# First expert weights, cleared sums and tables issued from the second scored tile of the first routing on

## Chip, cores and metric

The kernel runs on one core of one Trainium2 chip. The metric is the device time of one execution in microseconds (us). Before the change it is 1562.98 us, the median of three runs (1562.39 to 1564.65).

## What is computed

The reference is a block of three parts on X of 4 x 512 tokens with 512 channels: a mixture of experts, attention, and the same mixture of experts again. Cut to what matters:

```python
x = x + 0.5 * ffn(layernorm(x))        # "layer 0"
x = x + attention(layernorm(x))        # attn has its own layernorm, rope and residual
x = x + 0.5 * ffn(layernorm(x))        # "layer 1", same weights
# ffn: scores = sigmoid(x @ gate_w); 4 of 8 groups, then 6 of 64 experts a token;
#      every expert takes at most 96 tokens; out = silu(x @ w_gate) * (x @ w_up) @ w_down
#      plus one shared expert for all tokens (ws_gate, ws_up, ws_down)
```

All of it is in float32. The 2048 tokens are 16 tiles of 128 rows, in 4 groups (one for each batch entry) of 4 tiles.

## The kernel before

Layer 0 has two stages: the routing, and the experts. The change lies in the first.

**Routing of layer 0** (lines 633 to 719). For each tile t a chain of small steps is issued, which the text below calls by one letter and the tile's number:

- `row` (L289): ScalarE writes the normalised tile xn (L295, two buffers), and SyncE stores it to the DRAM table xn_d (L297). A third `row` needs a buffer whose store has landed.
- `turn` (L300): TensorE transposes xn (L201), ScalarE copies the result out as xT (L202).
- `score` (L305): TensorE multiplies by the gate weights (L308), ScalarE applies tanh (L313, tile lgs).
- `choose(g)` (L315): a chain of some 40 small VectorE instructions for the four tiles of a group, from sb (L323) to the weights wt (L397). wt shares the buffer of sb, so the next group's sb (L323) waits until SyncE has stored wt(g) to xn_d (L516).
- `count`, `digits`, `tokens`, `spread` (L400 to L458): they turn the choice into slot lists; TensorE's L447 needs VectorE's V and A (L423, L427).
- `gate`, `turn_h`, `down` (L477, L494, L502): the shared expert; TensorE L208, ScalarE L211, VectorE L214 and L215, TensorE L508, VectorE L509.

The routing begins with a first loop of nine rounds (lines 653 to 667), each `row(t)`, `turn(t)`, `score(t-1)`, with `choose(0)` after score 3. Then comes the main loop (lines 694 to 716): in each of its 15 rounds it runs the shared expert of one tile, the first steps of a tile two groups ahead, and one entry of a list of steps, which starts with choose(1), count(0) and spread(0, 0). At its end `finish` (L460) makes the index table en (L475).

**Loads ahead of the experts.** `rest` holds 15 DMAs of 768 KB, the weights of the first five pairs of experts (L250 to L252). `more` holds 20 entries: 17 for cleared blocks of the sums (L229, 256 KB each; the last entry also clears the last rows of xn_d and more of the sums, L231 to L234) and three tables for the attention (L671 to L673). `some(1)`, called at the end of each round of the main loop, takes one of each; after the loop `some(len(more))` takes what is left.

**Experts of layer 0** (L519). GpSimd gathers each expert's 96 rows from xn_d by en with an indirect DMA (L526), so the first gather needs every store to xn_d and en. TensorE transposes them (`turn(e)`, L201), and for each pair of experts multiplies by the weights (L549 to L555, then L568 and L571). The first pair's L549 is issued after `turn(0)` to `turn(3)`. A pair's weights are reloaded five pairs ahead, as soon as its buffer is free; results are added to the sums in DRAM by GpSimd (L576).

**What sets the order.** In this stretch TensorE's and SyncE's instructions stand in the order of the program (manual_schedule, L599 and L635). Those of ScalarE, VectorE and GpSimd are ordered when the kernel is built, by a scheduler that goes by its own estimate of when each instruction would be ready; on the chip each engine then runs its list strictly in that order. All of SyncE's DMAs go through one queue, and each waits at SyncE for the data that it stores, and for the DMA eight places earlier to land.

Of the kernel before, what the change touches and what calls it, by code (L numbers as in the profile page):

```python
# [17 lines left out]
P = 128  # L18
B, S, D = 4, 512, 512
T = B * S  # L20
NT = T // P
# [15 lines left out]
WS, WX = 2, 3  # L37
# [46 lines left out]
def macaron_kernel(ctx: ExitStack, tc: tile.TileContext, X, ln_w, ln_b, W_in, W_out, gate_w, bias,  # L84
                   w_gate, w_up, w_down, ws_gate, ws_up, ws_down, rope, out):
    nc = tc.nc
# [18 lines left out]
    lnw_b = const.tile([P, D], F32, name="lnw_b")  # L105
    lnb_b = const.tile([P, D], F32, name="lnb_b")
    rope_sb = const.tile([P, TPB, 2 * ROT], F32, name="rope_sb")
# [119 lines left out]
    def clear(layer, tiles):  # L227

        done = [nc.sync.dma_start(total[layer][1][t * P:(t + 1) * P, :], zero[:, :D]).ins for t in tiles]  # L229
        if NT in tiles:  # L230
            done.append(nc.sync.dma_start(xn_d[layer][T:T + P, :], zero).ins)  # L231
            if layer == 0:
                done.append(nc.sync.dma_start(total[layer][0][T:T + P, :], zero[:, :D]).ins)
                done += [nc.sync.dma_start(total[layer][0][t * P:(t + 1) * P, :], zero[:, :D]).ins  # L234
                         for t in range(NT - TPB, NT)]
        return done
# [4 lines left out]
    def load_pair(layer, n, extra):  # L241


        slot = (extra if (n + (0 if layer else WS)) % (WS + WX) >= WS else wp).tile([P, 4608], F32, tag="w", name="w")
        wg = slot[:, 0:2 * DC * F].rearrange("p (t c f) -> p t c f", t=2, c=DC)
        wu = slot[:, 2 * DC * F:4 * DC * F].rearrange("p (t c f) -> p t c f", t=2, c=DC)
        wd = slot[:, 4 * DC * F:].rearrange("p (k d) -> p k d", k=3)
        two = slice(2 * n, 2 * n + 2)
        loaded[layer, n] = (wg, wu, wd)
        return [lambda: nc.sync.dma_start(wg, w_gate[two].rearrange("t (p c) f -> p t c f", c=DC)),  # L250
                lambda: nc.sync.dma_start(wu, w_up[two].rearrange("t (p c) f -> p t c f", c=DC)),
                lambda: nc.sync.dma_start(wd, w_down[two].rearrange("t f d -> (t f) d").rearrange("(k p) d -> p k d", p=P))]  # L252
# [367 lines left out]
    def load_win(k):  # L620

        if k % 2 == 0:
            slot = wp.tile([P, 4608], F32, tag="w", name="w")
            win.extend(slot[:, h * DC * D:(h + 1) * DC * D].rearrange("p (c f) -> p c f", c=DC) for h in range(2))
        nc.sync.dma_start(win[k], (W_out if k == 3 else W_in[:, k * D:(k + 1) * D]).rearrange("(c p) f -> p c f", p=P))


    with ExitStack() as s:
        extra = s.enter_context(tc.tile_pool(name="wx0", bufs=WX))
        psA = s.enter_context(tc.tile_pool(name="psA", bufs=2, space=bass.MemoryType.PSUM))  # L630
        psB = s.enter_context(tc.tile_pool(name="psB", bufs=2, space=bass.MemoryType.PSUM))
        psD = s.enter_context(tc.tile_pool(name="psD", bufs=4, space=bass.MemoryType.PSUM))
        with ExitStack() as f:
            rp = f.enter_context(tc.tile_pool(name="rp0", bufs=2))
            f.enter_context(tc.manual_schedule(engines={mybir.EngineType.SP}))  # L635
            xs = []
            for t in range(NT):
                g, i = divmod(t, TPB)
                x = xp.tile([P, D], F32, tag=f"x{i}", name=f"x{i}")
                nc.sync.dma_start(x, X[t * P:(t + 1) * P, :])  # L640
                if i == 0:
                    xs.append([])
                xs[g].append(x)
                if t == TPB - 1:
                    nc.sync.dma_start(wsgu[:, 0], ws_gate.rearrange("(p c) f -> p c f", c=DC))
                    nc.sync.dma_start(wsgu[:, 1], ws_up.rearrange("(p c) f -> p c f", c=DC))
                    nc.sync.dma_start(wsd, ws_down.rearrange("(c p) d -> p c d", p=FH))
            route0 = route = Route(0)
            route.use(rp, psA, psD, 2)
            route.xp = rp, 2 * TPB  # L650
            route.begin(0, xs[0])

            for t in range(2 * TPB + 1):
                g, i = divmod(t, TPB)
                if t == TPB - 1:
                    with tc.issue_after(route.begun):
                        route.begin(1, xs[1])
                if g < 2:
                    route.row(g, xs[g], i)
                    route.turn(g, i)  # L660
                if t > 0:
                    route.score(*divmod(t - 1, TPB))
                if t == TPB:
                    for later in range(2, B):
                        with tc.issue_after(route.begun):
                            route.begin(later, xs[later])
                    route.choose(0)

            rest = [go for n in range(WS + WX) for go in load_pair(0, n, extra)]
            more = [lambda t=t: clear(0, (t,)) for t in range(NT + 1)]  # L670
            more += [lambda: nc.sync.dma_start(rope_sb, rope.rearrange("(i p) c -> p i c", p=P)),  # L671
                     lambda: nc.sync.dma_start(lnw_b, ln_w.partition_broadcast(P)),
                     lambda: nc.sync.dma_start(lnb_b, ln_b.partition_broadcast(P))]  # L673

            def some(n):
                for todo in (rest, more):
                    for _ in range(min(n, len(todo))):
                        todo.pop(0)()

            def spread(g, i):  # L680
                route.tokens(g, i)
                route.spread(g, i)
                if i == 0:
                    route.digits(g, 2)

            def count(g):
                route.count(g)
                route.digits(g, 0)

            steps = [lambda: route.choose(1), lambda: count(0), lambda: spread(0, 0), lambda: spread(0, 2), None,  # L690
                     lambda: (route.choose(2), count(1)), lambda: spread(1, 0), lambda: spread(1, 2), lambda: count(2),
                     None, lambda: (route.choose(3), spread(2, 0)), lambda: spread(2, 2), lambda: count(3),
                     lambda: spread(3, 0), lambda: spread(3, 2)]
            for g in range(B - 1):
                ahead = g + 2 if g + 2 < B else None
                if ahead:
                    route.row(ahead, xs[ahead], 0)
                if g + 2 == B - 1:
                    route.xp = late, TPB
                for i in range(TPB + 1):  # L700
                    if i > 0:
                        route.turn_h(g, i - 1)
                    if i < TPB:
                        route.gate(g, i)
                        if ahead:
                            route.turn(ahead, i)
                            route.score(ahead, i)
                            if i + 1 < TPB:
                                route.row(ahead, xs[ahead], i + 1)
                    step = steps.pop(0)  # L710
                    if step:
                        step()
                    route.store()
                    some(1)
                    if i > 0:
                        route.down(g, xs[g], i - 1)
            route.finish()
            route.store()
            some(len(more))
        def also(n):  # L720
            for k in range(2 * n - E + 6, 2 * n - E + 8):
                if 0 <= k < 4:
                    load_win(k)

        experts(0, route.en, extra, psA, psB, psD, also)


    with ExitStack() as s:
# [147 lines left out]
        rest = (1.0, lambda: None)  # L876
# [221 lines left out]
    with ExitStack() as s:  # L1098
        extra = s.enter_context(tc.tile_pool(name="wx1", bufs=WX))
# [81 lines left out]
```

## Time and profile before

| what | value |
|---|---|
| median of three runs | 1562.98 us |
| the profiled execution's own time | 1569.51 us |
| its span | 1567.8 us |
| TensorE busy / VectorE / ScalarE / GpSimd, of the span | 90% / 40% / 38% / 22% |
| first loop of the routing | about 14 to 41 us |
| main loop of the routing, to en (L475) | about 41 to 144.4 us |
| first gather (L526) issued | 150.73 us |
| first expert's L549 begins | 162.60 us |
| experts of layer 0 end | about 454 us |

The profile is one execution, 1.8 us around the span included in its own time. In the views below, a row of the timeline is: start in us, duration in us, engine, line, operation, output and input, shapes, count; in brackets the idle time of the engine before it and what ended it. PE is TensorE's matmuls, PEld its weight loads, DVE VectorE, ACT ScalarE, POOL GpSimd, and SPq the issue of DMAs by SyncE. A row of the windows gives, for a stretch of time, its length, the busy time and number of instructions of PE, PEld, DVE, ACT and POOL, the granted clock of TensorE, the share of time that the 16 DMA engines were busy, and GB/s.

### The profile page before, as it was taken

The numbers are of one execution on the slowest core, as the hardware profiler recorded it, in microseconds if no ns is written. First come the engines' busy times: TensorE is split into PE (matmuls) and PEld (weight loads), VectorE is DVE, ScalarE is ACT, GpSimd is POOL, SyncE is SP. The second block draws the span as 40 slices with busy tenths as digits, with TensorE's granted clock in tenths as the row PEclk, the third lists the DMA queues.
The fourth block names the chain that finished last, engine by engine and source line by source line (L and its number), as shares of the span: only waits on it lengthen the run. The fifth ranks groups of instructions, "written<-read, shape, count | busy, mean of one in ns | idle before, by whom it ended". The sixth has DMA issues, their size and how long they took to land.

```text
span 1567.8 us, 23011 instructions
## 1 busy us (share of the span) xinstructions
PE 1407.9 (90%) x9024; PEld 803.2 (51%) x9024; DVE 625.0 (40%) x1572; ACT 594.5 (38%) x1161; POOL 350.7 (22%) x321
## 2 busy tenths in 40 slices
PE   4785999999998998999999999978998899999990
PEld 4553777776753443334443434324334477777760
DVE  7575222211217566177144843375316422122110
ACT  4431121211112487668635774467362112121120
POOL 2001355545434000000000000000000245555535
PEclk9998899999999997999999998986798799999995
DMA  5477699999999300000000020000006389999989
GB/s 195 142 227 256 188 330 330 328 334 337 337 274 176 122 1 1 1 1 1 27 31 1 1 74 21 24 14 20 25 1 240 122 266 333 336 337 328 338 253 122
DMA packets 127036, 254.57 MB, mean 162 GB/s; under 512 B 15801, under 2 KB 32313, under 8 KB 126929
## 3 DMA queue, kind: packets, MB, share of 16 engines
q1 hardware_dynamic: 87216, 192.96, 35.1%
q0 software_dynamic: 39424, 59.97, 17.9%
q8 instruction: 72, 1.18, 0.3%
q14 instruction: 36, 0.29, 0.1%
q10 hardware_dynamic: 288, 0.16, 0.0%
HBM read 202.21 MB, written 56.95 MB: 165 GB/s over the span
## 4 chain that ended last, share of the span: by engine, by line
PE 56%; ACT 5%; DVE 4%; DMA 2%; issue 2%; POOL 1%; SPq 0%; POOLq 0%; ACTq 0%; DVEq 0%
PE pq L811 10%; PE gu L549 6%; PE sct L992 5%; PE sc L962 4%; PE cx L1015 4%; PE sct L996 4%; PE ps_t L201 4%; PE po L860 3%; PE eo L568 3%; PE gu L208 3%; PE so L508 3%; PE gu L553 3%; ACT sc L970 2%; PE eo L571 2%; DMA w<-in_L_ffn_w_up_dram 1%
## 5 line engine op out<-in xcount | busy, mean ns | idle before, releaser
L526 POOL DMA_INDIRECT xr<-xn_d,en x128 | 119.5, 934 | 893.7 <-DVE sg L215 721.2
L549 PE MATMUL gu<-bT,w 128*128 128x96 f32 x2048 | 245.1, 278 | 7.5 <-DMA w<-in_L_ffn_w_up_dram 7.3
L549 PEld LDWEIGHTS gu<-bT,w 128*128 128x128 f32 x2048 | 238.3, 194 | 10.3 <-issue 10.2
L970 ACT ACTIVATE sc<-sc,nmq 128x512 f32<-128x512 f32 x256 | 168.9, 660 | 58.2 <-DVE nmq L965 52.5
L811 PE MATMUL pq<-w,lT 128*128 128x512 f32 x384 | 177.1, 608 | 6.6 <-ACT lT L202 2.7
L965 DVE TENSOR_REDUCE nmq<-sc 128x2 f32<-128x1024 f32 x128 | 151.4, 1220 | 78.3 <-PE sc L962 78.2
L576 POOL DMA_INDIRECT total<-ob,en x96 | 138.6, 1443 | 159.3 <-ACT ob L575 120.4
L575 ACT ACTIVATE ob<-eo,xr 96x512 f32<-96x512 f32 x128 | 80.5, 678 | 185.9 <-PE eo L571 182.6
L560 DVE SCALAR_TENSOR_TENSOR sg<-sg,gu 128x288 f32<-128x288 f32 x64 | 29.0, 454 | 298.6 <-ACT sg L559 204.5
L1003 ACT ACTIVATE pT<-sct 128x1024 f32<-128x1024 f32 x128 | 124.1, 1023 | 58.1 <-PE sct L996 57.9
L559 ACT ACTIVATE sg<-gu 128x288 f32<-128x288 f32 x64 | 26.2, 410 | 314.4 <-PE gu L555 310.5
L568 PE MATMUL eo<-w,hT 128*96 128x512 f32 x256 | 125.3, 612 | 0.0
L202 DVE COPY bT<-ps_t 128x384 f32<-128x384 f32 x128 | 65.5, 552 | 147.4 <-PE ps_t L201 127.3
L811 PEld LDWEIGHTS pq<-w,lT 128*128 128x128 f32 x384 | 70.8, 193 | 95.9 <-issue 79.5
L962 PE MATMUL sc<-kT,qT 32*128 32x512 f32 x512 | 98.1, 719 | 10.4 <-ACT sc L970 9.8
L553 PE MATMUL gu<-bT,w 128*64 128x96 f32 x1024 | 99.9, 252 | 0.0
L555 PE MATMUL gu<-bT,w 128*64 128x96 f32 x1024 | 99.9, 252 | 0.0
L208 PE MATMUL gu<-wsgu,xT 128*128 128x384 f32 x256 | 94.8, 518 | 1.4 <-ACT ob L575 1.4
L992 PE MATMUL sct<-qT,kT 32*128 32x512 f32 x512 | 91.3, 659 | 2.1 <-ACT pT L1003 2.1
L553 PEld LDWEIGHTS gu<-bT,w 128*64 128x64 f32 x1024 | 87.7, 139 | 6.2 <-issue 0.3
L555 PEld LDWEIGHTS gu<-bT,w 128*64 128x64 f32 x1024 | 87.7, 139 | 0.0
L996 PE MATMUL sct<-nmT,pick 4*128 4x512 f32 x512 | 85.4, 614 | 0.0
(162 smaller groups left out, 1649.5 us busy)
## 6 DMA issues: line engine op xcount, KB each, us to landing
w<-in_L_ffn_w_gate_dram SPq DMA_DIRECT2D x64, 768.0 KB
w<-in_L_ffn_w_up_dram SPq DMA_DIRECT2D x64, 768.0 KB
w<-in_L_ffn_w_down_dram SPq DMA_DIRECT2D x64, 768.0 KB
total<-zero SPq DMA_DIRECT2D x39, 256.0 KB
xn_d<-xn SPq DMA_DIRECT2D x32, 256.0 KB
x<-in_L_attn_X_dram SPq DMA_DIRECT2D x16, 256.0 KB
x<-total POOLq DMA_DIRECT2D x16, 256.0 KB
out_dram<-x SPq DMA_DIRECT2D x16, 256.0 KB
```

Source lines behind the costliest of these rows:

```text
L208: nc.tensor.matmul(gu[:rows, :2 * F].rearrange("p (w f) -> p w f", w=2), lhsT=bT[:, c, :], rhs=weights[:, :, c, :], start=c == 0, stop=c = ...
L549: nc.tensor.matmul(g[:, k, :], lhsT=w[:, k, c, f:f + P], rhs=x[:, c, :], start=c == 0, stop=c == DC - 1)
L553: nc.tensor.matmul(g[:FC, 2, :], lhsT=w[:, 0, c, P:F], rhs=xa[:, c, :], start=c == 0, stop=c == DC - 1)
L555: nc.tensor.matmul(g[FC:, 2, :], lhsT=w[:, 1, c, 0:FC], rhs=xb[:, c, :], start=c == 0, stop=c == DC - 1)
L568: nc.tensor.matmul(eos[k][:CAP], lhsT=hT[:, k, :], rhs=wd[:, 2 * k, :], start=True, stop=False)
L576: nc.gpsimd.indirect_dma_start(out=total[layer][k], in_=ob, in_offset=None, out_offset=bass.IndirectOffsetOnAxis(ap=en[:, e:e + 1], axis=0 ...
L811: nc.tensor.matmul(pq, lhsT=lTs[i][:, c, :], rhs=win[n][:, c, :], start=c == 0, stop=c == DC - 1)
L962: nc.tensor.matmul(scs[j // 2][:, j % 2, :], lhsT=qT[b][rows, c, q * P:(q + 1) * P], rhs=kT[b][rows, c, :], start=True, stop=True)
L965: nc.vector.tensor_reduce(nmv[:, q, 2 * pair:2 * pair + 2, c], scs[pair], AX.X, ALU.max, negate=True)
L970: nc.scalar.activation(scs[j // 2][:, j % 2, :], scs[j // 2][:, j % 2, :], AF.Exp, bias=nmq[:, q, j * DH + c:j * DH + c + 1], accum_out=sm ...
L992: nc.tensor.matmul(scs[j // 2][:, j % 2, :], lhsT=kT[b][rows, c, kt * P:(kt + 1) * P], rhs=qT[b][rows, c, :], start=True, stop=False)
L996: nc.tensor.matmul(scs[j // 2][:, j % 2, :], lhsT=pick[rows, c, :], rhs=nmT[b][c // (NC - 1)][rows, :], start=False, stop=True)
```

## The change

`rest`, `more` and `some` are defined ahead of the first loop, and `some(1)` is also called in the first loop, after each score:

```diff
             route0 = route = Route(0)
             route.use(rp, psA, psD, 2)
+
+            rest = [go for n in range(WS + WX) for go in load_pair(0, n, extra)]
+            more = [lambda t=t: clear(0, (t,)) for t in range(NT + 1)]
+            more += [lambda: nc.sync.dma_start(rope_sb, rope.rearrange("(i p) c -> p i c", p=P)),
+                     lambda: nc.sync.dma_start(lnw_b, ln_w.partition_broadcast(P)),
+                     lambda: nc.sync.dma_start(lnb_b, ln_b.partition_broadcast(P))]
+
+            def some(n):
+                for todo in (rest, more):
+                    for _ in range(min(n, len(todo))):
+                        todo.pop(0)()
+
             route.xp = rp, 2 * TPB
             route.begin(0, xs[0])
...
                 if t > 0:
                     route.score(*divmod(t - 1, TPB))
+                    some(1)
...
                     route.choose(0)
-
-            rest = [go for n in range(WS + WX) for go in load_pair(0, n, extra)]
-            more = [lambda t=t: clear(0, (t,)) for t in range(NT + 1)]
-            more += [lambda: nc.sync.dma_start(rope_sb, rope.rearrange("(i p) c -> p i c", p=P)),
-                     lambda: nc.sync.dma_start(lnw_b, ln_w.partition_broadcast(P)),
-                     lambda: nc.sync.dma_start(lnb_b, ln_b.partition_broadcast(P))]
-
-            def some(n):
-                for todo in (rest, more):
-                    for _ in range(min(n, len(todo))):
-                        todo.pop(0)()
```

No instruction is added or removed. What moves, as the two built kernels list their instructions:

- **SyncE.** Before: 10 stores of xn, two of wt, then one weight load and one cleared block among each few stores, and 8 cleared blocks and 3 tables at the very end. After: eight weight loads and eight cleared blocks stand between the stores of xn 1 and xn 8; seven loads are left behind the stores of wt, and all cleared blocks and tables stand ahead of the store of the ninth output tile (x_178).
- **ScalarE.** Before (rows xn, copies xT, tanh lgs): xn2 xn3 xT2 lgs1 xn4 xT3 lgs2 xn5 xT4 lgs3 xT5 lgs4 xn6 xn7 xT6 lgs5 xT7 lgs6 xn8 lgs7 xn9 sg0 xT8 xn10 lgs8 hT0 sg1 ... After: xn2 xn3 xT2 lgs1 xT3 lgs2 xn4 xT4 lgs3 xn5 xT5 lgs4 xn6 xT6 lgs5 xn7 xT7 lgs6 lgs7 xn8 sg0 xT8 lgs8 hT0 xn9 sg1 xT9 lgs9 hT1 xn10 xn11 sg2 ... (sg and hT are the shared expert's L211 and L202.)
- **VectorE.** Before, the start of choose(1) (L323) follows the first shared product (L214, L215) and wt(0). After, wt(0) precedes that product, and L323 follows the products of tiles 0 and 1 and the first output tile (L509); next behind L323 is the product of tile 2 (L214), and behind that the rest of choose(1).
- **TensorE, GpSimd**: the same order.

## Prediction

> **What bounds the kernel now.** I read the page's slices first, then the timeline where the routing passes into the experts, then backwards the first 65 us on each engine, and last one-microsecond windows around the gathers. The slices of PE and DMA:
>
> ```profile
> PE   4785999999998998999999999978998899999990
> ...
> DMA  5477699999999300000000020000006389999989
> ```
>
> The fourth slice (118 to 157 us) is the hole that the change aims at: PE at 0.5, DMA at 0.6. The timeline there:
>
> ```profile
> 144.15 0.22 DVE L475 SCALAR_TENSOR_TENSOR en<-pt,none 96x64 uint32<-96x64 f32 x1
> 144.81 1.34 SPq L231 DMA_DIRECT2D xn_d<-zero  x1
> 146.79 2.72 SPq L234 DMA_DIRECT2D total<-zero  x4
> 151.09 0.44 SPq L673 DMA_DIRECT2D lnb_b<-in_L_attn_ln_b_dram  x1
> 150.73 1.19 POOL L526 DMA_INDIRECT xr<-xn_d,en  x1 [134.14 <-DMA total<-zero]
> 159.51 3.29 PE L201 MATMUL ps_t<-ident,xr 96*128 96x96 f32 x16 [16.26 <-issue]
> 162.60 6.35 PE L549 MATMUL gu<-bT,w 128*128 128x96 f32 x32
> ```
>
> The index is ready at 144.37, but the first gather waits 6.4 us more for cleared rows of xn_d that are queued behind other cleared blocks, and its rows are usable 8.75 us after it starts. From en to the first L549 it takes 18.2 us. Everything later hangs on that start: from 162.6 to about 300 us PE is full, a pair of experts takes 8.77 us, and the first reload of a weight buffer goes out at 179.26, when pair 0 is done. Later in the stage PE waits for weights only 5.4 us in all. A shift of the first L549 therefore moves the end one for one.
>
> **What is gained behind the routing.** After the change nothing but the stores of the last output tiles is left on SyncE's queue at the end, so the first gather follows en as in layer 1, where the queue is empty: en ends at 1225.39, and
>
> ```profile
> 1226.29 1.03 POOL L526 DMA_INDIRECT xr<-xn_d,en  x1 [721.21 <-DVE sg L215]
> ```
>
> that is 0.9 us later. Its rows (96 x 576 x 4 bytes = 221 KB) pass here:
>
> ```profile
> 1227.00:1228.00 1.00, 1.00 (x3) 0.50 (x2) 0.00 (x0) 0.50 (x2) 0.70 (x2) 0.50 0.00 0
> 1228.00:1229.00 1.00, 1.00 (x2) 0.34 (x1) 0.00 (x0) 0.00 (x0) 0.69 (x2) 0.50 0.81 221
> ```
>
> All 221 KB have moved by 1229.0, 2.7 us after the gather began; with half a microsecond for the signal I take 3.2 us. Gathers start 1.27 us apart, so the fourth (for turn(3), which stands before the first L549) starts 3.8 us after the first; turn(3) at half clock adds 0.8. Sum from en to the first L549: 0.9 + 3.8 + 3.2 + 0.8 = 8.7 us instead of 18.2, a **gain of 9.5 us**. The bounds: if the 8.75 us belonged to a first gather as such, L549 would wait 5.5 us more (gain 4); below 2.7 us it can't be by that row. A rule speaks for doubt here: by the Trainium skill, "DMA: Bandwidth & Descriptors", section Queues, rings and completion order, each DMA engine alternates between the queues that have work, so SyncE's backlog could only about double the 0.6 us that 221 KB take, and clearing it would bring about 0.6 us instead of the 5.5. The row says 8.75 against 2.7; in 151 to 156 us the engines moved only 102 to 167 GB/s, while the two broadcast tables were on their way. These tables go out earlier after the change, so I go by layer 1's row. The clock brings nothing: PE stands idle for some 5 us before the gathers land instead of 16, and the granted clock had fallen 4.1 us into the idle time (143.3 to 147.4), so the first L549 runs at half clock as now.
>
> **What is lost inside the routing.** The order lists move, and I follow them with the durations of before. First loop:
>
> ```profile
> 32.94 0.22 ACT L313 ACTIVATE lgs<-lg 128x64 f32<-128x64 f32 x1 [1.01 <-PE lg L308]
> 33.06 2.32 ACT L295 ACTIVATE xn<-x,off,rs 128x512 f32<-128x512 f32 x2
> ...
> 34.38 1.12 PE L201 MATMUL ps_t<-ident,xn 128*128 128x128 f32 x4 [1.47 <-ACT xn L295]
> ```
>
> Wherever ScalarE's xn(t) stands behind lgs(t-2), PE runs dry: score ends at 32.71, the next turn begins at 34.38, 1.67 us lost. Before, this happens for tile 6 alone of tiles 4 to 7 (xn4 and xn5 stand one place earlier, xn7 goes with xn6). After, xn4, xn5, xn6 and xn7 all stand so: 3 x 1.67 = **5.0 us** later for the end of the first loop and for the first gate (41.05 becomes 46.05). A round is then 0.86 + 1.60 + 1.67 = 4.1 us.
>
> Next, VectorE:
>
> ```profile
> 47.78 0.42 DVE L397 TENSOR_TENSOR wt<-wt,den 128x256 f32<-128x256 f32 x1
> 50.29 0.42 DVE L323 SCALAR_TENSOR_TENSOR sb<-lgs,bias_h 128x256 f32<-128x256 f32 x1 [2.08 <-DMA xn_d<-wt]
> 51.32 0.35 DVE L214 SCALAR_TENSOR_TENSOR sg<-sg,gu 128x192 f32<-128x192 f32 x1 [0.61 <-ACT sg L211]
> 55.12 0.69 DVE L509 SCALAR_TENSOR_TENSOR x<-so,x 128x512 f32<-128x512 f32 x1 [0.22 <-PE so L508]
> ...
> 64.07 0.95 DVE L427 TENSOR_TENSOR A<-hv,digit_a 128x1536 bf16<-128x1536 bf16 x1
> 65.07 0.34 PE L447 MATMUL o<-V,A 128*96 128x128 bf16 x1 [4.97 <-DVE A L427]
> ```
>
> From the product at 51.32 on VectorE is full until A ends at 65.02, and PE waits 4.97 us for it: here VectorE's chain sets the pace. After the change choose(1) stands behind the L509 of tile 0, which was at 55.12 and comes at 60.1, and then behind the product of tile 2. That tile's gate ends at 57.7 before, 62.7 after; ScalarE's sg2 now stands behind xn10 and xn11 (from 60.8 a pair takes 2.3 us, to 63.1) and ends at 63.4. So the chain that began at 51.32 begins at 63.5, 12.2 us later. It is shorter by what now precedes it: L509 with its wait, 0.83 us, and one product, 0.4. A ends at 63.5 + 13.7 - 1.2 = 76.0 instead of 65.0, **11.0 us later**. The wait for wt(0) (2.08 us above) no longer counts: its store stands behind xn9 in SyncE's queue, xn9 is done at about 55.2, and 55.3 + 0.5 + 2.1 = 57.9 is before 60.8.
>
> From A on the lists of PE, VectorE and ScalarE are the same but for trifles, PE waits there only in pieces of at most 1.84 us, and all of these hang on the same chain; so I carry the 11.0 us to en: 144.4 becomes 155.4. Bounds: PE waited 4.97 us for A, so the 5.0 us of the first loop could have been absorbed, if the 12.2 us did not come on top (loss then 6); and loads that are no longer in the way later (in 64 to 144 us ScalarE waited about 2 us for stores of xn) may give back up to 2. I take 11.0.
>
> **The moved DMAs.** A round's load and cleared block and store are 1.31 MB. Where the kernel now runs just this mix it moves 403 to 420 GB/s (70 to 78 us), so 3.2 us a round, under the 4.1 us that ScalarE's order asks for. The store of xn4 then lands at about 32.4, and xn6 takes its buffer at 36.6; nobody waits. On SyncE the eight loads stand ahead of stores of xn which aren't ready earlier, and their issue of 0.4 to 0.5 us each fits a round. The next seven loads stay behind the store of wt(1) (63.6 before, 74.6 after) as now and land before 140. In 50 to 63 us the DMA engines idle before and after. GpSimd has nothing queued but the gathers. Price: nothing, with the cover above; if it goes, see the second rival.
>
> **Sum.** 11.0 lost less 9.5 gained: first L549 at 155.4 + 8.7 = 164.1 instead of 162.6, **1.5 us later**, and the first reload at 180.8 instead of 179.3. The experts stage has the same transfers from there, attention and layer 1 are unchanged. The profiled execution would take 1569.5 + 1.5 = 1571.0 us; it lay 6.5 us above the median, so the median becomes 1563.0 + 1.5 = **1564.5 us**. About 0.2% (3.1 us) is what a measurement of this kernel can tell from no change.
>
> **The rivals.**
> 1. *The routing keeps most of its pace.* If the lists cost only part of the 11 us, because TensorE warms up earlier or the five microseconds of slack at 60 us take up the first loop's loss, en comes at 147 to 150 and L549 at 156 to 159: 4 to 7 us faster, 1556 to 1559. At the extreme, en at 144.4 as now, it is 9.5 us faster, 1553.5. For it: the wait of 4.97 us. Against it: both places where choose(1) now stands are in the list, and VectorE executes it in order.
> 2. *Slower: the early loads hold up xn.* xn(t+2) needs the landing of the store of xn(t), which sits in one queue behind 1.05 MB of load and cleared block. It decides once a round's 1.31 MB take more than 4.1 us, below 320 GB/s. The X tiles came at 365 to 391 GB/s, but in 64 to 66 us, when such a burst starts, only 113 GB/s moved at a DMA share of 0.99. At 250 GB/s a round takes 5.2 us, 1.1 too much, over six rounds 6.6 us: 1571. A gather as slow as now ends in the same place: 5.5 us on top, 1570.
> 3. *It moves nothing in effect.* SyncE must still wait for wt(1) with seven loads behind it, and the queue would be as full at the end as now. Then only the loss stays, 11 us, 1574. Against it: the last clears and tables stand ahead of four stores of x that follow late rounds.
>
> **How the numbers follow.** Forecast (within about 3 us of 1564.5, own range 1561 to 1568) 0.5; rival 1 0.18; rival 2 0.27; rival 3 0.05. Of the forecast's half, some 0.1 lies beyond 1566.1. So faster by over 0.2% 0.18, within 0.2% 0.40, slower 0.42. The range takes rival 1 to 1557 and rival 2 to 1572.
>
> **What would show it.** In the profile after: the turns of tiles 4 to 7 each behind a wait for ScalarE's xn, the first gate (L208) near 46; choose(1)'s L323 near 61 and PE's wait before the first L447 near 10 us, A near 76; en near 155; no cleared block or table issued after it; the first gather about 1 us behind en and the first L549 8 to 9 us behind; the first reload near 181. It is wrong if en stays below 151 (rival 1), if ScalarE's xn waits for xn_d in the first loop (rival 2), or if the first transpose still comes 8 us after the first gather.

## The result and the profile after

The changed kernel took 1581.78 us, median of 20 executions (1564.31 to 1594.53). The kernel before, run between them, took 1566.9 us (20 executions, 1557.19 to 1584.88). The ratio is 1.0076, with a 95% interval of 1.0053 to 1.0099: some 0.8% slower, where 0.1% was forecast. The ratios here leave out slow runs, those over 1.5% above the fastest of their kernel (over 1587.8 us for the changed kernel, over 1580.5 for the one before), and so this one doesn't compare like with like; the groups below do.

Both sets of times fall into two groups. I part them at 1577 us:

| batch | kernel | executions | lower group: number, median | upper group: number, median |
|---|---|---|---|---|
| first | before | 20 | 14, 1564.91 | 6, 1584.03 |
| first | changed | 20 | 7, 1568.53 | 13, 1584.21 |

Within a group the kernels lie 0.2 to 3.6 us apart. Most of the 15 us between the two medians comes from how many executions fell into each group, so there are two questions: did the routing and the tail do what was forecast, and what makes the groups?

**The routing and the tail.** The profile after is an execution of 1584.37 us (span 1582.6), against 1569.51 (1567.8) before. First loop, the turn of tile 7 in the timeline of the changed kernel:

```profile
41.16 0.22 ACT L313 ACTIVATE lgs<-lg 128x64 f32<-128x64 f32 x1 [1.01 <-PE lg L308]
41.28 1.25 ACT L295 ACTIVATE xn<-x,off,rs 128x512 f32<-128x512 f32 x1
42.59 1.12 PE L201 MATMUL ps_t<-ident,xn 128*128 128x128 f32 x4 [1.46 <-ACT xn L295]
```

The row xn starts as soon as lgs is done, and TensorE waits 1.46 us for it. The turns of tiles 4, 5 and 6 show the same wait (1.46 to 1.48 us). Then VectorE's list, and TensorE's wait for A:

```profile
59.96 0.69 DVE L509 SCALAR_TENSOR_TENSOR x<-so,x 128x512 f32<-128x512 f32 x1 [3.05 <-PE so L508]
60.57 0.42 DVE L323 SCALAR_TENSOR_TENSOR sb<-lgs,bias_h 128x256 f32<-128x256 f32 x1
63.12 0.35 DVE L214 SCALAR_TENSOR_TENSOR sg<-sg,gu 128x192 f32<-128x192 f32 x1 [2.14 <-ACT sg L211]
74.69 0.95 DVE L427 TENSOR_TENSOR A<-hv,digit_a 128x1536 bf16<-128x1536 bf16 x1
75.69 0.34 PE L447 MATMUL o<-V,A 128*96 128x128 bf16 x1 [10.75 <-DVE A L427]
```

The choice of group 1 (L323) starts right behind the addition L509 of tile 0, at 60.57 where it stood at 50.29 before, and TensorE's wait for A has grown from 4.97 to 10.75 us. The tail:

```profile
154.83 0.22 DVE L475 SCALAR_TENSOR_TENSOR en<-pt,none 96x64 uint32<-96x64 f32 x1
156.04 1.19 POOL L526 DMA_INDIRECT xr<-xn_d,en  x1 [139.20 <-DMA total<-x]
159.60 0.87 PE L201 MATMUL ps_t<-ident,xr 96*128 96x96 f32 x4 [5.68 <-issue]
164.09 5.88 PE L549 MATMUL gu<-bT,w 128*128 128x96 f32 x32
```

No cleared block stands behind en now. The gather goes out 1.0 us after it and its rows are used 3.6 us later, where it took 6.4 and 8.75 before. So the first L549 comes at 164.09, 1.5 us later than before.

Where the 8.75 us went shows in the DMA queues. Before, from the gather's start at 150.73 to 155.7 us only packets of SyncE's queue move, 867 of them, at 138 GB/s: the gather's first packet comes 5.0 us after its start. In the changed kernel it comes 1.9 us after (157.94). The broadcast tables were under way in those 5 us; whether they or the cleared blocks kept the gather's packets back, no run separates.

**Where the rest arises.** I matched the two profiles matmul by matmul (9024 in each). The changed kernel is 1.0 to 1.6 us late from 164 to 336 us, 2 to 6 at 627 to 829, 4.1 at 855 to 943, 15.9 from 981 to 1060, and 14.5 at the end: nearly 12 us are lost between 940 and 980 us, in the attention's context of the third batch element, which the change doesn't touch. The windows there, of the kernel before:

```profile
940.00:950.00 10.00, 10.00 (x47) 4.33 (x40) 0.38 (x2) 5.42 (x8) 0.00 (x0) 0.51 0.07 26
950.00:960.00 10.00, 10.00 (x78) 5.28 (x77) 0.58 (x1) 5.80 (x10) 0.00 (x0) 1.00 0.08 28
960.00:970.00 10.00, 10.00 (x63) 4.16 (x63) 6.52 (x25) 4.25 (x7) 0.00 (x0) 1.00 0.00 1
```

and of the changed kernel:

```profile
940.00:950.00 10.00, 9.46 (x50) 4.33 (x48) 0.95 (x5) 5.75 (x9) 0.00 (x0) 0.67 0.05 20
950.00:960.00 10.00, 10.00 (x47) 4.46 (x40) 0.00 (x0) 3.81 (x5) 0.00 (x0) 0.50 0.10 36
960.00:970.00 10.00, 10.00 (x47) 4.31 (x45) 0.00 (x0) 3.49 (x6) 0.00 (x0) 0.50 0.00 1
```

PE is "busy" for 9.46 to 10 of the 10 us in all six rows. What differs from 950 us on is the granted clock (third number from the end) and the matmuls done: 78 and 63 at 1.00, 47 and 47 at 0.50. By the clock's records this half-clock stretch lasts 10.24 us before (from 939.5) and 37.55 us after (from 943.4). At half speed the 27.3 us more would lose at most 13.7 us; nearly 12 were lost. A half-clock step of the context, in the timeline of the changed kernel (in its code the attention stands one line further down, L993 for L992):

```profile
953.84 1.97 PE L308 MATMUL lg<-gw,xT 128*128 128x64 f32 x8
955.74 2.09 PE L993 MATMUL sct<-qT,kT 32*128 32x512 f32 x8
957.61 1.93 PE L997 MATMUL sct<-nmT,pick 4*128 4x512 f32 x8
959.47 1.11 PE L201 MATMUL ps_t<-ident,xn 128*128 128x128 f32 x4
```

Most of its time goes to matmuls that use 32 or 4 of the 128 rows (L993, L997) or 32 of the columns (L1016, which follows). The stretch ends at 980.95, during the first gate L208 (128 x 128, 384 elements) that comes by:

```profile
976.55 1.94 PE L1016 MATMUL cx<-pT,v 128*32 128x512 f32 x8
978.41 4.09 PE L208 MATMUL gu<-wsgu,xT 128*128 128x384 f32 x8
982.43 1.14 PE L993 MATMUL sct<-qT,kT 32*128 32x512 f32 x8
```

After it the same eight L993 take 1.14 us instead of 2.09. The same holds in every profile that has such a stretch of over 30 us in the context of the second or third batch element (seven in all): it ends when four of a gate's eight matmuls have begun. The stretches of 10 to 14 us there end without a gate.

### The profile page after: what moved, and what is told of

It reads as the page before. It is cut to its first block, busy times and chain, and to the rows that moved or that the text cites. A ratio compares the mean times of both kernels' runs of the same rounds, so it can differ in the third digit from the quotient of the medians.

```text
span 1582.6 us, 23002 instructions
## 1 busy us (share of the span) xinstructions
PE 1422.0 (90%) x9024; PEld 805.9 (51%) x9024; DVE 626.0 (40%) x1572; ACT 594.9 (38%) x1161; POOL 350.8 (22%) x321
## 4 chain that ended last, share of the span: by engine, by line
PE 57%; ACT 4%; DVE 3%; DMA 3%; issue 2%; POOL 1%; POOLq 0%; SPq 0%; ACTq 0%; DVEq 0%
PE pq L812 10%; PE gu L549 6%; PE sct L993 5%; PE sc L963 5%; PE cx L1016 4%; PE sct L997 4%; PE ps_t L201 4%; PE gu L208 3%; PE eo L568 3%; PE po L861 3%; PE so L508 3%; PE gu L553 2%; PE eo L571 2%; ACT sc L971 2%; DMA w<-in_L_ffn_w_up_dram 1%
## 5 line engine op out<-in xcount | busy, mean ns | idle before, releaser
L549 PE MATMUL gu<-bT,w 128*128 128x96 f32 x2048 | 243.9, 277 | 9.3 <-DMA w<-in_L_ffn_w_up_dram 9.3
L549 PEld LDWEIGHTS gu<-bT,w 128*128 128x128 f32 x2048 | 236.8, 193 | 12.4 <-issue 12.3
L576 POOL DMA_INDIRECT total<-ob,en x96 | 138.6, 1443 | 155.7 <-ACT ob L575 112.7
L202 DVE COPY bT<-ps_t 128x384 f32<-128x384 f32 x128 | 65.6, 552 | 136.3 <-PE ps_t L201 136.3
L208 PE MATMUL gu<-wsgu,xT 128*128 128x384 f32 x256 | 95.8, 523 | 1.4 <-ACT ob L575 1.4
L993 PE MATMUL sct<-qT,kT 32*128 32x512 f32 x512 | 93.5, 694 | 2.1 <-ACT pT L1004 2.1
L997 PE MATMUL sct<-nmT,pick 4*128 4x512 f32 x512 | 86.6, 642 | 0.0
```

Of the source, the lines that this page charges most:

```text
L208: nc.tensor.matmul(gu[:rows, :2 * F].rearrange("p (w f) -> p w f", w=2), lhsT=bT[:, c, :], rhs=weights[:, :, c, :], start=c == 0, stop=c = ...
L549: nc.tensor.matmul(g[:, k, :], lhsT=w[:, k, c, f:f + P], rhs=x[:, c, :], start=c == 0, stop=c == DC - 1)
L576: nc.gpsimd.indirect_dma_start(out=total[layer][k], in_=ob, in_offset=None, out_offset=bass.IndirectOffsetOnAxis(ap=en[:, e:e + 1], axis=0 ...
L993: nc.tensor.matmul(scs[j // 2][:, j % 2, :], lhsT=kT[b][rows, c, kt * P:(kt + 1) * P], rhs=qT[b][rows, c, :], start=True, stop=False)
L997: nc.tensor.matmul(scs[j // 2][:, j % 2, :], lhsT=pick[rows, c, :], rhs=nmT[b][c // (NC - 1)][rows, :], start=False, stop=True)
```

## The experiments

**Theory A**: the change costs what the forecast says, about 1.5 us. The groups are made by half-clock stretches in the attention, which any execution of either kernel may catch. **Theory B**: the change shifts the attention so that it catches them more often. **Theory C**: a cost of some 12 us is paid in every execution.

### The changed kernel again, three times

No edit.

> The changed kernel once more, unaltered. Theory A (the change itself costs 1.5 us: 11.0 lost in the routing, 9.5 won behind it; the other 13 us of the profiled difference come from a stretch of some 40 us at half clock in the attention, which any execution of either kernel may catch): the single times fall again into a group at 1564 to 1573 and one at 1579 to 1595, the kernel before into one at 1557 to 1570 and one at 1577 to 1585; within a group the kernels differ by 1 to 4 us, and the share of the upper group changes from batch to batch for both. Theory B (the shift of 1.5 us places the attention so that the long half-clock stretch is caught more often): the upper group holds two thirds of the changed kernel's times again, and a third or less of those before. Theory C (a cost of 12 us that is paid in every execution): no time below 1575. In the profile A and B expect the matmuls of the experts 1.5 us later than before, to within 0.3; any larger shift appears only where the granted clock differs.

> The changed kernel once more, one profiled execution. Theory A: if the execution is of the lower group (1561 to 1575), its profile has no half-clock stretch of over 30 us between 740 and 1110 us and PE's matmuls there stand 1 to 6 us later than in the profile of before; if it is of the upper group (1579 to 1595), it has at least one such stretch and the distance to before jumps by 10 us or more inside it. A jump without a lowered clock, or a time of the upper group without such a stretch, would refute it.

> The changed kernel a third time, for the share of its times in the upper group (1577 and over), which was 13 of 20 in the first batch and 6 of 22 in the second; the kernel before had 6 of 20, 17 of 65, 3 of 11 and 8 of 37. Theory A (the share is none of the change's doing): about a quarter, 3 to 8 of some 20, a lower group at 1561 to 1575 with a median 2 to 4 us above that of the kernel before. Theory B (the change raises the share): half or more, 10 to 14 of 20, as in the first batch. A share between these (9 of 20) leaves it open.

Measured, with the kernel before in the same batches and in those of the experiments below:

| batch | kernel | lower group: number, median | upper group: number, median |
|---|---|---|---|
| second | changed (after_again) | 16, 1567.40 | 6, 1583.07 |
| second | before | 49, 1565.10 | 16, 1582.62 |
| fifth | changed (after_third) | 14, 1567.33 | 8, 1583.44 |
| fifth | before | 20, 1565.15 | 7, 1581.83 |
| all | changed | 37, 1567.61 | 28, 1583.78 |
| all | before | 120, 1565.05 | 40, 1582.51 |

The ratios of these two batches are 1.0044 (1.0017 to 1.0072) and 1.0019 (0.9990 to 1.0048). Theory C falls: of the changed kernel's 65 executions 37 lie below 1577, down to 1560. Between the lower groups of all batches lie 2.6 us (0.3 to 3.7, from resampling the times), against a forecast of 1.5. Of theory B the strong form (two thirds again) falls: the upper group's share in these two batches is 14 of 44 for the changed kernel, and 34 of 140 for the kernel before outside the first batch; such a difference comes up by chance one time in three. The first batch's 13 of 20 did not come back. But a weaker theory B stays open: with the first batch counted in, 28 of 65 stand against 40 of 160, which chance gives one time in a hundred, and all four profiled executions of the changed kernel, each the first of its batch, were of the upper group (1584.37 to 1584.69 us). The first batch raised the question, so it can't also answer it. The batches ran on different chips; in each of them the kernel before shows both groups. after_look (1584.46 us) has its long stretch elsewhere, 41 us from 763.9 in the context of the second batch element, as theory A allows. The mean clock goes with the group: 0.931 to 0.944 in after_third's lower group, 0.920 to 0.929 in its upper. The experts' first L549 comes at 164.04 us in after_again, as in the first profile.

### Dense matmuls in the attention

```diff
                 scs = [psS.tile([P, 2, S], F32, tag="sc", name="sct") for _ in range(2)]
+                if b == 2 and (c, kt) in ((0, 1), (0, 2), (0, 3), (1, 0)):
+                    for _ in range(2):
+                        nc.tensor.matmul(scs[0][:, 0, :], lhsT=kT[b][:, c, kt * P:(kt + 1) * P],
+                                         rhs=qT[b][:, c, :], start=True, stop=True)
                 for j in range(HG):
```

That is after_dense. In before_dense2 and after_dense2 the condition is `b in (1, 2)`, and `sums` has eight matmuls of the same shape for b == 3, at (c, q) of (1, 3), (2, 0), (2, 1), (2, 2).

> The changed kernel with eight matmuls of 128 rows x 128 columns x 512 elements added at the start of the attention's context of the third batch element (two ahead of the scores at each of four steps; they write a tile that the next matmul overwrites, so the output is unchanged). They cost 8 x 0.5 = 4 us at full clock, up to 8 at half. Theory A and B: dense work of that kind ends a half-clock stretch, as the shared expert's gates L208 do at 980 us in the changed kernel's profile; so no half-clock stretch of over 15 us begins between 935 and 960 us, the lower group stays 3 to 5 us above that of the changed kernel (1569 to 1573), and the upper group loses most of its distance: some 1575 instead of 1583, the rest of it from the stretch at 1060 to 1100, which this doesn't touch. If the clock is lowered there for another reason than the sparse matmuls, the stretch of 37 us stays and the times are 4 to 8 us above the changed kernel's in both groups. Theory C: plus 4 to 8 us throughout.

> The kernel before with 24 added matmuls of 128 rows x 128 columns x 512 elements, at the three places where a half-clock stretch of 37 to 41 us has appeared in some profile (context of the second and of the third batch element, row sums of the fourth; eight each, two ahead of the scores at each of four steps; they write a tile that the next matmul overwrites, so the output is unchanged). Eight such cost 3.6 us in the lower group of times, so 24 cost 8 to 12. If the two groups of times are made by these stretches (theory A's second half), none of over 25 us starts at these places in the profile and the times close up: lower end 1567, median 1574 to 1577, at most one in ten above 1583. If the groups come from something else (another execution-wide cause that the clock only follows), the split stays: a quarter or more of the times lie 15 us or more above the median of the rest, near 1590 to 1595.

> The changed kernel with the same 24 dense matmuls at the same places. Theory A: the groups close up as in the kernel before with these matmuls, and the difference of the two medians is what the change itself costs, 1 to 4 us (1576 to 1580 against 1574 to 1577). Theory B (the change raises the share of the long stretches through its shift): the difference also closes, but then the changed kernel without the added matmuls must have shown a higher share in every batch, which the last batch (6 of 22 against 17 of 65) didn't. Theory C (a cost of 12 us in every execution, hidden in the last batch by chance): 12 us between the two medians.

Measured: after_dense 1573.89 us median of 14. They leave no clear gap: parted at 1580, which allows for the added matmuls, 10 have a median of 1570.99 and 4 lie above; parted at 1577, 9 have one of 1570.30. before_dense2 1568.95 (1556.74 to 1573.63, 6 executions); after_dense2 1571.62 (1565.74 to 1577.11, 6). The window from 930 to 990 us, in the changed kernel, then in the kernel before, then in after_dense:

```profile
930.00:990.00 60.00, 59.22 (x255) 26.08 (x253) 10.25 (x37) 24.64 (x40) 0.00 (x0) 0.69 0.14 53
```

```profile
930.00:990.00 60.00, 59.22 (x326) 26.34 (x324) 16.59 (x63) 27.21 (x41) 0.00 (x0) 0.91 0.17 63
```

```profile
930.00:990.00 60.00, 59.76 (x337) 26.33 (x335) 18.86 (x70) 28.81 (x49) 0.00 (x0) 1.00 0.16 58
```

The eight matmuls cost 2.9 to 3.6 us in the lower group (against 1567.40), and in this profile the window has no half clock: 337 matmuls. That alone proves little, since the execution is of the lower group, where the window is slow for 10 us at most (326 matmuls before). The upper group stays, with 4 of 14 above 1580, where I expected some 1575; other places of the stretch would explain it, but no profile of after_dense shows one. The stronger test is the other two kernels. With all three places covered, neither profile has a half-clock stretch of over 11 us between 740 and 1190 us, and none of 12 executions lies in an upper group (the highest is 1577.11, 3 us above the next of its kernel, where the groups otherwise lie 15 us apart); at the rate of the kernel before, a quarter, that would happen 3 times in 100 (0.75 to the 12th). The shift in time that the added matmuls bring isn't what removes the group: in the profile of rest_only (below) the attention stands some 8 us later and in that of more_twice some 8 us earlier than before, and both kernels keep it. The 24 matmuls cost less than expected, net of what they save: the medians lie 5 and 4 us below the lowest I gave, some 4 above the lower groups without them. The two kernels then differ by 2.7 us: the change alone, as far as six executions of each can tell.

### The two parts of the change, and a better place

rest_only calls in the first loop

```diff
                     route.score(*divmod(t - 1, TPB))
+                    if rest:
+                        rest.pop(0)()
```

more_only the same with `more`, and more_twice, an edit of the kernel before, leaves the first loop alone and takes two of `more` in each round of the main loop:

```diff
                     route.store()
                     some(1)
+                    if more:
+                        more.pop(0)()
```

> The changed kernel, but its first loop issues only the weight entries; cleared blocks and tables are issued from the second loop on, one a round, and the remainder at the end, as before. It should have the loss without the gain: the first gate L208 at 46.8 us, A at 75.6, en at 155.0 as in the changed kernel, and the first L549 18.2 us after en, near 173, so the experts 10.5 to 11 us later than before. If the cleared blocks and not the weights make the loss, en is near 144 to 150. For the time: theory A 1577 in the lower group and 1593 in the upper, both present; theory B the same groups, shares open; theory C (12 us in every execution, from the weight loads) would give 1590 or more even in the lower group.

> The changed kernel, but its first loop issues only cleared blocks and tables; the weight loads are issued from the second loop on, as before. In ScalarE's list the row xn then stands behind lgs in two of the four rounds of the first loop instead of four, and VectorE's choice ahead of the shared expert's additions as before. My theory of the routing (its loss is the place of these instructions in the lists, 1.67 us for each xn behind an lgs) gives half of the loss in the first loop and little behind it: the first gate L208 at 43 to 45 us at the clock of the kernel before (46.8 in the changed kernel, 41.05 before), en at 147 to 150 (155.0; 144.4), and the first L549 8.7 to 9.1 us later, at 156 to 159: 4 to 6 us earlier than before, time some 1561 in the lower group. If the loss is the transfers of cleared blocks on SyncE's queue ahead of the rows' stores, en is near 155 as in the changed kernel and the time near 1567.

> more_only once more, for its time. Theory A: lower group at 1555 to 1559, 7 to 10 us below the kernel before, an upper group at 1573 to 1578 with a fifth to a third of the times, ratio to the kernel before 0.993 to 0.996. If the earlier times of 1555 were luck of the clock in the first 150 us, the lower group lies at 1559 to 1563, no better than the kernel before with two cleared blocks a round.

> The kernel before, with two cleared blocks or tables issued in each round of the second loop instead of one; the weight loads and the first loop are as before. All my theories of the change's two parts expect the routing as before (the index en ready at 144.4 us in the profile, the first expert gate L549 then 8.7 us later, near 153, against 162.6) and the experts 9.5 us earlier than before. If tail and routing aren't additive (the rows of the first gather are late for another reason than SyncE's backlog), L549 is near 162. For the time: theory A 1557 to 1559 in the lower group and about 1574 in the upper, with both groups present; theory B the same groups, with a share that may be anything, since the shift is -9.5 us; theory C no change from before, since its cost lies elsewhere.

| kernel | turns of tiles 4 to 7 that wait 1.46 to 1.48 us for xn | first gate L208 | A done | en | first L549 | lower group | upper group |
|---|---|---|---|---|---|---|---|
| before | 1 | 41.05 | 65.0 | 144.4 | 162.6 | 1565.05 | 40 of 160 |
| changed | 4 | 46.81 | 75.6 | 155.1 | 164.1 | 1567.61 | 28 of 65 |
| rest_only | 3 | 45.95 | 73.7 | 153.0 | 169.8 | 1571.99 | 7 of 20 |
| more_only | 2 | 42.97 | 64.7 | 140.9 | 150.1 | 1555.46 | 1 of 4 |
| more_only_again | 2 | 43.32 | 66.1 | 144.5 | 153.6 | 1554.64 | 6 of 16 |
| more_twice | 1 | 37.41 | 60.8 | 139.9 | 149.0 | 1558.12 | 5 of 23 |

(Times in us. The last two columns go by the gap in each kernel's own times.) The weight loads make most of the loss, and the cleared blocks make the gain. rest_only has the changed kernel's late A and a slow tail, though its queue is shorter at the end than before (16.7 us from en to L549 instead of 18.2), so it loses 7 us where I expected 10.5. more_only pays for one more wait at the first gate (1.9 to 2.3 us later), but VectorE's choice stays ahead of L509 (L323 at 48.19), and A is on time. Its tail, in the timeline of more_only:

```profile
140.69 0.22 DVE L475 SCALAR_TENSOR_TENSOR en<-pt,none 96x64 uint32<-96x64 f32 x1
141.91 1.19 POOL L526 DMA_INDIRECT xr<-xn_d,en  x1 [125.31 <-DMA w<-in_L_ffn_w_down_dram]
145.52 0.87 PE L201 MATMUL ps_t<-ident,xr 96*128 96x96 f32 x4 [5.73 <-issue]
150.10 6.04 PE L549 MATMUL gu<-bT,w 128*128 128x96 f32 x32
```

From en to L549 it takes 8.8 to 9.2 us in every kernel whose queue is empty by then, 18.2 before. more_twice beats both kernels (1559.17 us, median of 23; ratio to the kernel before 0.9947, 0.9927 to 0.9967), and so does more_only_again (1560.27, median of 16; 0.9961, 0.9927 to 0.9995). In more_twice and in both runs of more_only, en came earlier than I expected (by 2.5 us at least). The clock of these executions has a part in it: in more_twice its first record of full speed is at 26.8 us instead of 45.2, in more_only it fell once before 140 us instead of three times. (Ahead of the first record a row of the windows says 1.00, but the four L201 of a turn take 1.06 to 1.12 us there, and 0.60 after it.) How much of the gain that is, was not tested. The lead doesn't all reach the end: in its profile more_twice is 13.6 us early at the first L549, still 14.0 at 396 us, but 9.7 at 477, behind half-clock stretches from 406 and 467 us; its lower group lies 6.9 us below.

The profiles of more_only and more_only_again are one and the same kernel (on two chips) in both groups, 1578.1 and 1553.76 us. The windows of the first in the contexts of the second and third batch elements:

```profile
740.00:800.00 60.00, 59.22 (x250) 25.76 (x249) 11.75 (x40) 25.79 (x42) 0.00 (x0) 0.66 0.03 9
930.00:990.00 60.00, 59.22 (x320) 26.14 (x319) 16.98 (x67) 28.59 (x48) 0.00 (x0) 0.91 0.16 58
```

and of the second:

```profile
740.00:800.00 60.00, 58.38 (x312) 26.32 (x316) 18.56 (x67) 30.76 (x53) 0.00 (x0) 0.94 0.05 19
930.00:990.00 60.00, 59.83 (x358) 25.99 (x358) 20.62 (x69) 29.68 (x43) 0.00 (x0) 1.00 0.08 29
```

From 740 to 800 us the first does 250 matmuls at a clock of 0.66, the second 312 at 0.94. Matched matmul by matmul, the first loses 28 us between 752 and 1147 us, nearly all of it in half-clock stretches from 752.3, 943.4 and 1120.9 of 41.0, 10.2 and 27.3 us, and with no edit between the two. A stretch in the row sums isn't what makes the group: the fast profile has one too, 41 us from 1031.3, where TensorE waits for ScalarE anyway. Of the 13 profiled executions of all kernels, the 7 with a half-clock stretch of over 25 us in the context of the second or third batch element are of the upper group, and the 6 without are of the lower (more_twice's by the gap in its own times, after_dense's by 1577 or 1580).

### The same loads from another queue

```diff
                     route.score(*divmod(t - 1, TPB))
+                    onto[0] = nc.gpsimd
                     some(1)
+                    onto[0] = nc.sync
```

The rest of the edit makes `load_pair` issue its loads from `onto[0]`, which is `nc.sync` at the start.

> The changed kernel, but in its first loop the weight loads are issued on GpSimd's queue instead of SyncE's; from the second loop on they are on SyncE's again. The same bytes pass as early or earlier, but ScalarE's and VectorE's lists then stand as in more_only (two of four rows behind an lgs, the choice of the second batch element ahead of the shared expert's first addition). If the routing's loss is the order in these lists: first gate L208 at 43 to 45 us, en at 141 to 147, first L549 9 us later, time some 1556 to 1560 in the lower group. If the loss is the early transfers themselves (rows' stores or loads of x held up by 2.4 MB each): gate at 46 us or later and en at 152 to 157 as in the changed kernel, time 1567 or more. If GpSimd's issue of the loads delays the work of its own list, the transfers of x or the first rows are late: gate past 48 us.

Measured: 1564.3 us, median of 20 (14 below 1577, at 1562.92); ratio 0.9996 (0.9970 to 1.0023); en at 150.95, first L549 at 159.79. ScalarE's and VectorE's lists stand as in more_only, but GpSimd isn't paced by the scores and issues all eight loads from 16.9 to 23.1 us. A window of after_pool, and then its ScalarE's waits from 10 to 52 us (in total, times, longest):

```profile
35.00:40.00 5.00, 2.72 (x12) 2.53 (x12) 4.49 (x19) 1.50 (x2) 0.00 (x0) 1.00 1.03 415
```

```profile
ACT xn L297 <- DMA xn_d<-xn: 7.5, 4, 3.4
```

From 20 to 40 us the DMA engines are never free, at 406 to 415 GB/s: the rows' stores are late, xn waits 7.5 us for them (2.0 in the changed kernel, 1.7 before), and the first gate comes at 49.9, past the 48 of the third outcome given. So the first loop tests nothing of the lists here: it is the second rival, brought about by unpaced loads. Behind it the lists do show: A is done 22.8 us after the gate begins, 28.8 in the changed kernel, 24.0 before.

## Why the prediction was right and wrong

- **What failed**: in the step "Sum", the sentence "attention and layer 1 are unchanged". Their instructions are, but not their time, and the step put that at nothing without a reason. Executions of either kernel fall into two groups some 17 us apart (1565.05 and 1582.51 for the kernel before), parted by a long half-clock stretch in the attention, and 13 of the first batch's 20 were of the upper one. Of the 17.3 us between 1564.5 and 1581.78, some 12.7 are this, by what the next two terms leave over. Nothing in the profile of before said that it was one of two kinds of execution, but the row of 940 to 950 us at 0.51 with PE full was there to be seen, and a range for it would have reached to some 1585.
- **The other terms of the miss**: the starting point, the median of three runs, 1562.98, held no execution of the upper group; over 160 executions the kernel's median is 1566.51, 3.5 us higher. The change itself gives the last 1.1 (2.6 for 1.5).
- **Sum, +1.5 us**: right for the change itself: 1.5 at the first L549 and at the first reload (180.82), and 2.6 (0.3 to 3.7) between the lower groups; 2.7 with the long stretches broken up. That the first two came out to a tenth is partly luck: gain and loss each measured 0.3 less than forecast.
- **Tail, 9.5 us gained**: right, 9.2. From en to the first L549 it took 9.0 us (8.7 forecast). Layer 1's row was the better guide: the rows were used after 3.6 us (3.2 forecast).
- **The Trainium skill's rule on the queues** ("DMA: Bandwidth & Descriptors", section Queues, rings and completion order: a DMA engine takes turns among the queues that have work, a packet at a time): the 0.6 us drawn from it was my estimate for equal turns, and 5.2 us were measured (8.8 less 3.6). It was set aside rightly, but the rule isn't refuted: before, the gather had no packet moving for 5.0 us, so most of the time was lost ahead of any turns.
- **First loop, 5.0 us lost**: right. Four waits of 1.46 to 1.48 us; the gate at 46.8 (46.05 forecast). A round with the wait is 1.73 us longer than one without (1.67 forecast), 5.2 for three; the other 0.6 us is there at the turn of tile 2 already (23.40 against 22.83), and two runs of more_only differ there by 0.35 with no edit.
- **VectorE's list, A 11.0 us later**: right: 75.6 (76.0), en at 155.05 (155.4). rest_only and more_only part its cause: A is late where the choice stands behind L509, and on time where it doesn't.
- **Second rival**: not in this kernel (one wait of 2.0 us, 1.7 before), but real, as after_pool shows.
- **Small misreadings that changed nothing**: the fourth slice of the DMA row is 7, not 6; by the row shown, the score ends at 32.91; the clock fell at 147.6, not 147.4.

What stays open: why a stretch ends after 10 us in one execution and lasts until the next gate in another. Every length in the clock's records is a multiple of 3.413 us (3.41, 6.83, 10.24, 37.55, 40.96), and a half-clock step lasts 8.54 us (953.84 to 962.38), 2.5 times that, so each step may meet the clock's possible changes in the same places; this was not tried. Open too is why the changed kernel's first batch and its four profiled executions held so many long ones, and with it whether the change makes them somewhat more frequent.

## What to carry over

Look for stretches of a profile where the granted clock is down under a full PE before trusting a median of three: they can come and go from one execution to the next, and then a change of 2 us is only seen when groups of like clock are compared. When DMAs move to an earlier place, see what the scheduler does with the lists around them: here the shorter tail gained 9.2 us and the longer routing lost 10.7, and moving only the cleared blocks and tables gives 6 to 7 us by the medians. Pacing matters as much as the place: the same loads sent unpaced held up the rows.

## What was not expected of the hardware

- A TensorE that was busy without a gap (37.50 of the 37.50 us from 943.4 on) stayed at half clock for 37.5 to 41.0 us while its matmuls were mostly 32 rows, 4 rows or 32 columns wide; the 128 x 128 ones of a step (L201, 1.11 us, and L308, 1.97) didn't end it. All seven stretches ended in a gate, eight matmuls of 128 x 128 with 384 elements each; with eight of 512 elements added at each place, no such stretch stands in the two profiles, and the times of 12 executions show none.
- A long stretch in a context costs some 12 us (shift 4.1 to 15.9 across it), and none of that shows in PE's busy share: 59.22 of 60 us in the two windows of more_only, with 250 and 320 matmuls.
